# The shift layer of a four-layer network on one core: four positions per tile, its group norm computed once, its statistics taken inside the layer before

## The chip, the core and the metric

The kernel runs on one core of a Trainium2 chip (trn2). A core has a matrix engine (TensorE, PE in the profile; its weight loads are listed apart as PEld), a vector engine (VectorE, DVE), a scalar engine (ScalarE, ACT), a general engine (GpSimd, POOL) and a queue engine (SyncE, SP). SBUF is the on-chip memory of 128 partitions; PSUM is the memory that TensorE writes and that POOL does not read here. DMA transfers are issued by SP or ACT and run on 16 DMA engines that all queues share. The metric is the device time of one execution in microseconds; lower is better. All data is 32-bit floating point.

## What is computed

Eight images of 384 channels and 32 x 32 pixels pass through four residual layers. Layers 0 and 2 are selective state-space layers (layer 2 ends in an MLP), layer 1 is a deformable convolution. The change concerns layer 3, the shift layer, and the end of layer 2.

```python
def _gn(v, G=32, eps=1e-5):
    B_, C_, H_, W_ = v.shape
    g = v.reshape(B_, G, C_ // G, H_, W_)
    m = jnp.mean(g, axis=(2, 3, 4), keepdims=True)
    s = jnp.var(g, axis=(2, 3, 4), keepdims=True)
    return ((g - m) / jnp.sqrt(s + eps)).reshape(v.shape)

def _L3_conv_ref(x, offset):
    B, C, h, w = x.shape
    P = offset.shape[0]                      # 48 positions
    cpp = C // P                             # 8 channels each
    off_round = jnp.round(offset)
    off_int = off_round.astype(jnp.int32)
    disp = _displace(x.reshape(B, P, cpp, h, w), off_int).reshape(B, C, h, w)
    sub = offset - lax.stop_gradient(off_round)
    c = K // 2                               # K = 5, SIGMA = 0.5
    jj, ii = jnp.meshgrid(jnp.arange(K, dtype=jnp.float32) - c, jnp.arange(K, dtype=jnp.float32) - c, indexing='xy')
    field = jnp.stack([jj, ii], axis=-1)
    d = field[None] + sub[:, None, None, :]
    kernel = jnp.exp(-jnp.sum(d * d, axis=-1) / (2.0 * SIGMA ** 2))
    kernel = kernel / jnp.sum(kernel, axis=(1, 2), keepdims=True)
    kw = jnp.repeat(kernel, cpp, axis=0)[:, None]
    return lax.conv_general_dilated(disp, kw, (1, 1), [(c, c), (c, c)],
        feature_group_count=C, dimension_numbers=('NCHW', 'OIHW', 'NCHW'))

x = x + _L0_conv_ref(_gn(x), ...)
x = x + _L1_conv_ref(_gn(x), ...)
x = x + _L2_conv_ref(_gn(x), ...)
x = x + _L3_conv_ref(_gn(x), L3_conv_offset)
```

Each position has an offset (dx, dy) that its eight channels share. The channels are moved by the rounded offset, with zeros from outside, and then blurred with a 5 x 5 Gaussian centred on the fractional rest. Shift and blur along one axis are one 32 x 32 matrix, so a position needs two small matrices: one over y, one over x.

## The kernel before, in words

**Layer 2.** `ssm_layer` works through 16 steps, a half image each (`b`, `h`; 384 channels as three groups of 128 partitions, 512 pixels). A step is 48 units (six channel groups of the inner state by eight pairs of states). The order of ACT, PE, DVE and POOL is written out by hand: `plan` puts each operation into one of four queues at a unit number, and `run` issues them between the scans. SP is not in that list, so its transfers are ordered by the scheduler. The B and C rows of the next step come from DRAM in eight transfers of 1 MB (`load_bc`, L367) into eight buffers called `bc`, put at units 41 to 48. The MLP of a step runs among the units of the next one, except for the last step: there `out_proj`, `mlp_up`, `gelu` and `mlp_down` stand alone at the end of `ssm_layer`. `down_take` (L545, L547) adds the result to the residual `x` on DVE, and `store` (L504) writes the half image to DRAM after the third group. The weights of these products stream through three buffers `wm` (L246).

**Layer 3.** `shift_layer` opens new buffers and starts when layer 2 is done.
1. From the offsets it makes the rounded part, the fraction and the normaliser (L1402 to L1424).
2. For each of the eight images it loads `x` (L1432, two buffers), takes bn_stats of six 128 x 512 pieces (L111), aggregates (L125), and runs `gn_finish`: a product with `gmat` that averages the 12 channels of a norm group (L133), the deviations and their squares, a second product (L143), and Ln and Exp for the reciprocal root (L174, L175). The result is a scale and a shift per image and channel, `rn`.
3. Six products (L1444) spread scale and shift into `tab`, one value for each partition, image and channel slot.
4. In the loop over the 48 positions a tile `xr` holds one position: partition = (channel within a group of four, y), columns = (8 images, 2 channel groups, 32 x). It comes in two loads on SP of 128 KB (L1475) into three buffers. DVE scales and shifts it (L1481, two operations), TensorE multiplies four 128-column blocks of the data, as the stationary operand, with the block-diagonal matrix over y (L1490), which also turns the block; ACT copies the result out of PSUM (L1492); four more products do the x axis and turn it back (L1495); DVE adds it to `xr` (L1497); ACT issues two stores of 128 KB (L1500). The matrices of four positions at a time are built in the same loop on DVE and ACT (L1459 to L1468).

In DRAM the images lie as [image, channel, pixel], so loads and stores of a position move runs of 32 pixels, 128 bytes.

Of the kernel before, what the change touches and what calls it, by code (L numbers as in the profile page):

```python
# [8 lines left out]
F32 = mybir.dt.float32  # L9
# [75 lines left out]
class Net:  # L85
# [107 lines left out]
    def ssm_layer(self, li, src, dst):  # L193
# [3 lines left out]
        with ExitStack() as ctx:  # L197
# [292 lines left out]
            def residual(s):  # L490
                s["x"] = x = p2.tile([P, G, TS], F32, name="x", tag="x")
                nc.sync.dma_start(out=x, in_=src(s["b"])[:, :, s["sl"]])
# [9 lines left out]
            def store(s, o):  # L502
                if o == G - 1:
                    nc.sync.dma_start(out=dst(s["b"])[:, :, s["sl"]], in_=s["x"])  # L504
# [135 lines left out]
            with tc.manual_schedule(engines=ENGINES):  # L640
# [75 lines left out]
                residual(s)  # L716
                for o in range(G):
                    out_proj(s, o, 0, ND)
                    out_take(s, o)
                if mlp:  # L720
                    for q in range(NF // 4):
                        for f in range(4):
                            mlp_up(s, q, f)
                            up_take(s, q, f)
                        gelu(s)
                        for o in range(G):
                            mlp_down(s, q, o)
                            down_take(s, q, o)

# [653 lines left out]
    def shift_layer(self, src_of, src, dst):  # L1383
        tc, nc, ins = self.tc, self.nc, self.ins
        nb = self.nb
        NJ = CPP // IG
        NC4 = C // IG
        with ExitStack() as ctx:
            wp = ctx.enter_context(tc.tile_pool(name="w3", bufs=1))
            p2 = ctx.enter_context(tc.tile_pool(name="p2_3", bufs=2))  # L1390
            self.mm = ctx.enter_context(tc.tile_pool(name="mm3", bufs=3, space=PSUM))
            self.acc = ctx.enter_context(tc.tile_pool(name="acc3", bufs=3, space=PSUM))
            cst = wp.tile([P, T_D0 + W], F32, name="cst")
            nc.sync.dma_start(out=cst, in_=ins["c_l3"])
            off = wp.tile([P, NP, 2], F32, name="off")
            nc.sync.dma_start(
                out=off.rearrange("p n t -> p (n t)"),
                in_=ins["offset"].rearrange("n t -> (n t)").partition_broadcast(P),
            )

            offf = off.rearrange("p n t -> p (n t)")
            nc.vector.tensor_scalar(offf, offf, 4096.0, -4096.0, ALU.min, ALU.max)  # L1402
            rnd = wp.tile([P, NP, 2], F32, name="rnd")
            rndf = rnd.rearrange("p n t -> p (n t)")
            nc.vector.tensor_scalar(rndf, offf, ROUND, None, ALU.add)
            nc.vector.tensor_scalar(rndf, rndf, ROUND, None, ALU.subtract)
            sub = wp.tile([P, NP, 2], F32, name="sub")
            nc.vector.tensor_tensor(sub, off, rnd, ALU.subtract)
            norm = wp.tile([P, 2 * NP], F32, name="norm")
            tap = wp.tile([P, 2 * NP], F32, name="tap")  # L1410
            subf = sub.rearrange("p n t -> p (n t)")
            for t in range(-2, 3):
                nc.vector.tensor_scalar(tap, subf, float(t), None, ALU.add)
                nc.vector.tensor_tensor(tap, tap, tap, ALU.mult)
                dest = norm if t == -2 else tap
                nc.scalar.activation(dest, tap, AF.Exp, scale=-2.0)
                if t > -2:
                    nc.vector.tensor_tensor(norm, norm, tap, ALU.add)
            nc.vector.reciprocal(norm, norm)

            pos = wp.tile([P, 2 * NP], F32, name="pos")
            nc.vector.tensor_scalar(pos, rndf, self.col(Q_SRC + NT), None, ALU.add)
            nc.vector.scalar_tensor_tensor(norm, pos, 0.0, norm, ALU.is_ge, ALU.mult)
            nc.vector.scalar_tensor_tensor(norm, pos, float(W - 1), norm, ALU.is_le, ALU.mult)  # L1424
            grp = cst[:, T_GRP : T_GRP + IG]
            d0 = cst[:, T_D0 : T_D0 + W]


            rn = wp.tile([P, 2, nb, G], F32, name="rn")
            for b in range(nb):  # L1430
                x = p2.tile([P, G, L], F32, name="x", tag="x")
                nc.sync.dma_start(out=x, in_=src_of(b))  # L1432
                self.gn_stats(x, rn[:, 0, b, :], rn[:, 1, b, :])
            nq = P // IG
            hi = cst[:, T_HI : T_HI + nq].unsqueeze(1).to_broadcast([P, nb, nq])
            tab = wp.tile([P, 2, G, nb, nq], F32, name="tab")
            for t in range(2):
                for g in range(G):
                    sel = p2.tile([P, nb, nq], F32, name="sel", tag="sel")
                    nc.vector.tensor_tensor(  # L1440
                        sel, hi, rn[:, t, :, g].unsqueeze(2).to_broadcast([P, nb, nq]), ALU.mult
                    )
                    ps = self.psum("ps_tab", n=nb * nq)
                    nc.tensor.matmul(  # L1444
                        ps, cst[:, T_LO : T_LO + P], sel.rearrange("p b q -> p (b q)"), start=True, stop=True
                    )
                    nc.scalar.copy(tab[:, t, g].rearrange("p b q -> p (b q)"), ps)

            PC = 4
            for p0 in range(0, NP, PC):  # L1450
                M2 = 2 * PC
                e = p2.tile([P, M2, W], F32, name="e", tag="e")
                kr = p2.tile([P, M2, W], F32, name="kr", tag="kr")
                ef, krf = e.rearrange("p m w -> p (m w)"), kr.rearrange("p m w -> p (m w)")

                def rows(t):
                    return t[:, 2 * p0 : 2 * p0 + M2].unsqueeze(2).to_broadcast([P, M2, W])

                nc.vector.tensor_tensor(e, d0.unsqueeze(1).to_broadcast([P, M2, W]), rows(rndf), ALU.add)  # L1459
                nc.vector.tensor_tensor(kr, e, rows(subf), ALU.add)  # L1460
                nc.vector.tensor_tensor(krf, krf, krf, ALU.mult)
                nc.scalar.activation(krf, krf, AF.Exp, scale=-2.0)
                nc.scalar.activation(ef, ef, AF.Abs)
                nc.vector.scalar_tensor_tensor(krf, ef, 2.0, krf, ALU.is_le, ALU.mult)
                nc.vector.tensor_tensor(kr, kr, rows(norm), ALU.mult)
                bd = p2.tile([P, M2, IG, W], F32, name="bd", tag="bd")
                for i in range(IG):
                    nc.scalar.activation(bd[:, :, i, :], kr, AF.Copy, scale=grp[:, i : i + 1])  # L1468
                for n in range(PC):
                    p = p0 + n  # L1470
                    g, q = divmod(p * NJ, nq)
                    xr = p2.tile([P, nb, NJ, W], F32, name="xr", tag="xr", bufs=3)
                    for j in range(NJ):
                        c = p * CPP + j * IG
                        nc.sync.dma_start(  # L1475
                            out=xr[:, :, j, :],
                            in_=src[:, c : c + IG, :].rearrange("b i (y x) -> (i y) b x", x=W),
                        )
                    xa = p2.tile([P, nb, NJ, W], F32, name="xa", tag="xa")
                    for op, t in ((ALU.mult, 0), (ALU.add, 1)):  # L1480
                        nc.vector.tensor_tensor(  # L1481
                            xa, xr if t == 0 else xa,
                            tab[:, t, g, :, q : q + NJ].unsqueeze(3).to_broadcast([P, nb, NJ, W]), op,
                        )
                    xaf = xa.rearrange("p b j x -> p (b j x)")
                    my = bd[:, 2 * n + 1].rearrange("p i w -> p (i w)")
                    mx = bd[:, 2 * n].rearrange("p i w -> p (i w)")
                    ps = self.acc.tile([P, HL], F32, name="ps_y", tag="acc")
                    for k in range(0, HL, P):
                        nc.tensor.matmul(ps[:, k : k + P], xaf[:, k : k + P], my, start=True, stop=True)  # L1490
                    yt = p2.tile([P, HL], F32, name="yt", tag="yt")
                    nc.scalar.copy(yt, ps)  # L1492
                    ps2 = self.acc.tile([P, HL], F32, name="ps_yx", tag="acc")
                    for k in range(0, HL, P):
                        nc.tensor.matmul(ps2[:, k : k + P], yt[:, k : k + P], mx, start=True, stop=True)  # L1495
                    xrf = xr.rearrange("p b j x -> p (b j x)")
                    nc.vector.tensor_tensor(xrf, xrf, ps2, ALU.add)  # L1497
                    for j in range(NJ):
# [98 lines left out]
```

## Time and profile before

| | us |
|---|---|
| median of 3 runs | 9791.53 (9788.88 to 9793.73) |
| the profiled execution | 9790.55 |
| its span, first to last instruction | 9788.6 |
| last take of the last MLP ends | 9418.7 |
| last issue of a store ends | 9785.2 |

| engine | busy us | share of the span |
|---|---|---|
| PE | 8670.8 | 89% |
| DVE | 8165.1 | 83% |
| ACT | 6591.8 | 67% |
| POOL | 5655.4 | 58% |

Most of the span is layers 0 to 2, where several engines are nearly full at once. The rows used below come from views with these columns. In a windows view each row is a stretch of the span: its length, then the busy time of each engine with the number of instructions, the granted TensorE clock (1 is full speed), the mean busy share of the 16 DMA engines, and GB/s. In the chain of waits each row is a start time, a length and what the program's end was waiting for then. In a table of groups each row is a line, engine, operation, output<-input, shape and count, then total busy time, mean nanoseconds of one, and the idle time ahead of it with what ended it.

### The profile page before, as it was taken

The page shows a single profiled execution, that of the slowest core. Times are in us where ns is not written, and L with a number is a line of the kernel's source. Part 1 is how long each engine was busy: PE and PEld are TensorE (multiplying, and loading weights), DVE is VectorE, ACT ScalarE, POOL GpSimd, SP SyncE. Part 2 cuts the span into 40 slices and gives each one's busy share as a digit, 9 for nine tenths or more (in the row PEclk, how much of TensorE's full clock was granted, in tenths as well). Part 3 has the DMA queues.
Part 4 walks back from the last instruction along what each step waited for, and adds up shares of the span by engine and source line. Part 5 has one row for each costly group of instructions (what it writes and reads, how often), then busy time and mean ns, then how long its engine had stood idle before and what let it go on. Part 6 is the DMA issues. An engine that isn't in the chain of part 4 may idle for free. (4 is left out here: it accounts for less than half of the span.)

```text
span 9788.6 us, 89617 instructions
## 1 busy us (share of the span) xinstructions
PE 8670.8 (89%) x28965; PEld 4696.1 (48%) x28990; DVE 8165.1 (83%) x8959; ACT 6591.8 (67%) x10417; POOL 5655.4 (58%) x3740
## 2 busy tenths in 40 slices
PE   7888898888886999999999996899999999999876
PEld 2333333333333777767767774333344343443345
DVE  6999999999995778777877875999999999999834
ACT  5666666666663778777777775777767777677632
POOL 6888888888883000000000001999999999999900
PEclk8999999999998999999999997899999999999976
DMA  2211211211212333333333333222332223322226
GB/s 75 77 57 45 82 58 45 82 57 45 82 48 54 78 85 73 91 87 74 90 89 77 85 84 96 72 86 87 112 104 91 86 88 115 101 91 85 74 85 100
DMA packets 540008, 781.12 MB, mean 80 GB/s; under 512 B 231858, under 2 KB 372562, under 8 KB 515848
## 3 DMA queue, kind: packets, MB, share of 16 engines
q1 hardware_dynamic: 439688, 762.71, 26.4%
q10 hardware_dynamic: 99840, 12.59, 0.8%
q8 instruction: 231, 3.78, 0.2%
q14 instruction: 249, 2.04, 0.1%
HBM read 717.32 MB, written 57.87 MB: 79 GB/s over the span
## 5 line engine op out<-in xcount | busy, mean ns | idle before, releaser
L426 POOL TENSOR_TENSOR db<-du,bc 128x1024 f32<-128x1024 f32 x1536 | 3608.1, 2354 | 420.2 <-DVE hs L436 227.4
L436 DVE TENSOR_TENSOR_SCAN da<-da,db 128x1024 f32<-128x1024 f32 x1272 | 2912.3, 2290 | 200.1 <-ACT da L421 151.3
L467 PE MATMUL y<-hs,ident 128*128 128x512 f32 x5184 | 2611.1, 639 | 389.6 <-DVE hs L450 246.5
L421 ACT ACTIVATE da<-dt,na 128x512 f32<-128x512 f32 x3072 | 2120.2, 691 | 911.9 <-DVE hs L450 685.4
L394 POOL TENSOR_TENSOR dt<-dt,sp_e 128x512 f32<-128x512 f32 x192 | 243.8, 1270 | 3089.5 <-DVE sp_e L386 3089.5
L467 PEld LDWEIGHTS y<-hs,ident 128*128 128x128 f32 x5184 | 1018.6, 203 | 1877.6 <-issue 1138.4
L1370 PE MATMUL wacc<-fsm,fxk 128*128 128x221 f32 (+34 forms) x10624 | 1637.2, 312 | 73.4 <-DVE fsm L1340 71.6
L450 DVE TENSOR_TENSOR hs<-da,bc 128x1024 f32<-128x1024 f32 x1272 | 1558.0, 1225 | 117.7 <-PE y L467 14.1
L1370 PEld LDWEIGHTS wacc<-fsm,fxk 128*128 128x128 f32 x10624 | 1550.2, 193 | 210.2 <-DVE fsm L1340 132.6
L1340 DVE TENSOR_TENSOR fsm<-fhy,fhx 128x170 f32<-128x170 f32 (+42 forms) x3216 | 1174.2, 431 | 429.6 <-PE wacc L1370 414.1
L1300 ACT ACTIVATE fhy<-fpyx,cell 128x416 f32<-128x416 f32 (+9 forms) x1280 | 645.6, 576 | 397.9 <-DVE fsm L1340 397.9
L1058 PE MATMUL ps_off<-fxn,fow 128*32 128x248 f32 (+18 forms) x2944 | 832.7, 523 | 3.8 <-issue 2.0
L1323 DVE TENSOR_TENSOR fxk<-fxt,fwk 128x1024 f32<-128x1024 f32 (+1 forms) x688 | 787.5, 1182 | 6.3 <-ACT fxt L1116 6.3
L436 DVE TENSOR_TENSOR_SCAN hs<-da,db 128x1024 f32<-128x1024 f32 x264 | 602.4, 2282 | 67.7 <-POOL db L414 27.8
L447 POOL TENSOR_TENSOR hs<-hs,bc 128x1024 f32<-128x1024 f32 x264 | 621.7, 2355 | 38.0 <-ACT st L442 37.5
L454 POOL TENSOR_TENSOR hs<-hs 128x512 f32<-128x512 f32 x480 | 608.6, 1268 | 3.6 <-DVE hs L450 3.6
L538 PE MATMUL ps_m<-hid,wm 128*128 128x512 f32 x1152 | 540.4, 614 | 38.8 <-ACT hid L531 33.9
L521 PE MATMUL ps_h<-t,wm 128*128 128x512 f32 x1152 | 539.0, 606 | 15.0 <-DVE x L545 15.0
L1305 ACT ACTIVATE fhy<-fhy,cols 128x1344 f32<-128x1344 f32 (+10 forms) x368 | 530.7, 1442 | 12.0
L1058 PEld LDWEIGHTS ps_off<-fxn,fow 128*98 128x98 f32 (+2 forms) x2944 | 352.7, 147 | 382.2 <-issue 359.4
L442 ACT COPY st<-da 128x2 f32<-128x2 f32 x624 | 97.8, 157 | 504.4 <-DVE hs L450 503.0
L538 PEld LDWEIGHTS ps_m<-hid,wm 128*128 128x128 f32 x1152 | 222.2, 196 | 342.7 <-issue 263.6
(182 smaller groups left out, 9871.1 us busy)
## 6 DMA issues: line engine op xcount, KB each, us to landing
bc<-bcd SPq DMA_DIRECT2D x256, 1024.0 KB
fpyx<-fposd SPq DMA_DIRECT2D x640, 256.0 KB
wm<-in_w SPq DMA_DIRECT2D x96, 768.0 KB
x<-x SPq DMA_DIRECT2D x72, 768.0 KB
winr<-in_win SPq DMA_DIRECT2D x192, 192.0 KB
x<-in_x SPq DMA_DIRECT2D x40, 768.0 KB
fpyx<-fposd SPq DMA_DIRECT2D x24, 1024.0 KB
wm<-in_wout SPq DMA_DIRECT2D x48, 384.0 KB
```

What stands on the lines that cost most here:

```text
L421: nc.scalar.activation(da[:, i, :], s["dt", j], AF.Exp, scale=na[:, j, n : n + 1])
L426: nc.gpsimd.tensor_tensor(db, du, s["bc"][m][:, 0], ALU.mult)
L436: nc.vector.tensor_tensor_scan(h1, da1, db1, 0.0, ALU.mult, ALU.add)
L447: nc.gpsimd.tensor_tensor(s["hs", m], s["hs", m], c, ALU.mult)
L450: nc.vector.tensor_tensor(hs, s["da", m], c, ALU.mult)
L467: nc.tensor.matmul(s["y"], self.ident, s["hs", m][:, i, :], start=first and i == 0, stop=k == NU - 1 and i == n - 1,)
L538: nc.tensor.matmul(ps, s["w2"][:, f, o * P : (o + 1) * P], s["hid"][:, f, :], start=(f == 0), stop=(f == 3))
L1058: nc.tensor.matmul(o[:, ya - r0 : yb - r0, xa:xb], ow[:, (dy + pad) * K + dx + pad, :], x3[:, ya + dy : yb + dy, xa + dx : xb + dx], start ...
L1300: nc.scalar.activation(hy[:, at : at + (yb - ya) * W], pyx[:, 0, ya * W : yb * W], AF.Abs, bias=bias)
L1323: nc.vector.tensor_tensor(t[:, :n], x, wk[:, j : j + 1, :].to_broadcast([P, n, P]), ALU.mult)
L1340: nc.vector.tensor_tensor(self.sub(sm, at, [(r * w, n), (w, r), (1, w)]), self.sub(hy, hy_at[by] + xa, [(r * W, n), (W, r), (1, w)]), self ...
L1370: nc.tensor.matmul(a[:, ya - 4 * o : yb - 4 * o, xa:xb], k, self.sub(sm, sm_at[by], [(w, yb - ya), (1, w)]), start=False, stop=False,)
```

## The change

The shift layer is no longer a layer with its own buffers: `shift_parts` returns pieces that `ssm_layer` issues within its last MLP and after it, in the buffers of layer 2 (`bc`, `hs`, `db`, `u`, `xn`).

- `store` of layer 2 writes every third of a half image also to a new DRAM tensor `x3s` laid out [channel, y, image, x], in one transfer of 128 x 16 runs of 128 bytes; the old copy is written too, except in the last step.
- Ahead of the last `out_proj` six half images are loaded for the statistics; `kernels_a`, `kernels_b` and the bn_stats of 15 half images (five after each `gelu`) stand among the MLP's operations, and those of the last half image after each of its takes, from SBUF.
- `norms` does the two averaging products once, with the eight images side by side as columns, and builds `tab` with three products.
- A tile is now four positions: partition = (position, y), columns = (8 channels, 8 images, 32 x), 1 MB, loaded from `x3s` in four transfers of 1 KB runs. A chunk is half a tile, 128 x 1024. POOL multiplies by the scale; TensorE multiplies with the block-diagonal y matrix as the stationary operand and adds the shift as a second product of the same matrix with a broadcast row of the table; DVE transposes 32 x 32 blocks out of PSUM; TensorE does x; DVE transposes back; POOL adds. 32 stores of 32 KB a tile, half on SP, half on ACT.

The core of the diff, with the parts the text speaks of:

```diff
             def store(s, o):
-                if o == G - 1:
+                if mlp:
+                    y = s["h"] * H // 2
+                    nc.sync.dma_start(
+                        out=shift[0][o * P : (o + 1) * P, y : y + H // 2, s["b"] * W : (s["b"] + 1) * W],
+                        in_=s["x"][:, o, :].rearrange("p (y x) -> p y x", x=W),
+                    )
+                if o == G - 1 and (not mlp or s is not steps[-1]):
                     nc.sync.dma_start(out=dst(s["b"])[:, :, s["sl"]], in_=s["x"])
...
                 residual(s)
+                if mlp:
+                    load_consts()
+                    last = len(steps) - 1
+                    for i in range(6):
+                        stat_load(i)
+                    stats = list(range(last))
                 for o in range(G):
                     out_proj(s, o, 0, ND)
                     out_take(s, o)
                 if mlp:
+                    kernels_a()
...
                         gelu(s)
+                        if q == NF // 4 - 1:
+                            exp_ln()
+                        some(5)
+                        if q == 0:
+                            kernels_b()
                         for o in range(G):
                             mlp_down(s, q, o)
                             down_take(s, q, o)
+                            if q == NF // 4 - 1:
+                                stat(last, s["x"], o)
+                    for m in range(3):
+                        load(m)
+                    norms()
+                    main()
...
+        def bc(name, *shape):
+            t = ring("bc", [P, 2, 2, TS], name, NS // 2).rearrange("p a b l -> p (a b l)")
...
+        def load(m):
+            xr = d["xr", m] = bc("sxr", NI, W).rearrange("p (i w) -> p i w", w=W)
+            for n in range(IG):
+                c = (m * IG + n) * CPP
+                nc.sync.dma_start(
+                    out=xr[n * H : (n + 1) * H].rearrange("p (k b) w -> p k (b w)", k=CPP),
+                    in_=srcs[c : c + CPP].rearrange("k y b -> y k b"),
+                )
...
+        def scale(c):
+            m = c // 2
+            if c % 2 == 0:
+                d["xa", m] = bc("sxa", NI, W).rearrange("p (i w) -> p i w", w=W)
+            x, xa = (piece(d[k, m], c).rearrange("p (i w) -> p i w", w=W) for k in ("xr", "xa"))
+            nc.gpsimd.tensor_tensor(xa, x, table(c, 0).unsqueeze(2).to_broadcast([P, NI // 2, W]), ALU.mult)
+        def over_y(c):
+            ps = d["psy", c] = dap.tile([P, 2, TS], F32, name="ps_y", tag="da")...[:, :CH]
+            xa = piece(d["xa", c // 2], c)
+            for i in range(0, CH, HL):
+                o = ps[:, i : i + HL]
+                nc.tensor.matmul(o, mat(c, 1), xa[:, i : i + HL], start=True, stop=False)
+                t = table(c, 1)[:, i // W : i // W + HL // W].unsqueeze(2).to_broadcast([P, HL // W, W])
+                nc.tensor.matmul(o.rearrange("p (i w) -> p i w", w=W), mat(c, 1), t, start=False, stop=True)
+        def turn(c):
+            yt = d["yt", c] = ring("hs", [P, 2, TS], "syt", 4).rearrange("p a b -> p (a b)")
+            nc.vector.transpose(yt, d["psy", c])
+        def over_x(c):
+            d["psx", c] = []
+            for i in range(0, CH, HL):
+                ps = self.psum("ps_yx")
+                nc.tensor.matmul(ps, mat(c, 0), d["yt", c][:, i : i + HL], start=True, stop=True)
+                d["psx", c].append(ps)
+        def turn_back(c):
+            zt = d["zt", c] = ring("db", [P, 2, TS], "szt", 3).rearrange("p a b -> p (a b)")
+            for i, ps in enumerate(d["psx", c]):
+                nc.vector.transpose(zt[:, i * HL : (i + 1) * HL], ps)
+        def add(c):
+            m = c // 2
+            x = piece(d["xr", m], c)
+            nc.gpsimd.tensor_tensor(x, x, d["zt", c], ALU.add)
+            if c % 2:
+                for k in range(CPP):
+                    for n in range(IG):
+                        (nc.sync if n % 2 else nc.scalar).dma_start(
+                            out=dst[:, (m * IG + n) * CPP + k, :].rearrange("b (y x) -> y b x", x=W),
+                            in_=d["xr", m][n * H : (n + 1) * H, k * nb : (k + 1) * nb, :],
+                        )
+        def main():
+            nch = 2 * NM
+            for i in range(-3, nch):
+                for k, fn in ((3, scale), (2, over_y), (1, over_x), (2, turn), (1, turn_back), (0, add)):
+                    if 0 <= i + k < nch:
+                        fn(i + k)
+                m = i // 2 + 3
+                if i % 2 and 3 <= m < NM:
+                    load(m)
```

## Prediction

> **What bounds the kernel now.** I read the windows view by stage first, then the chain of waits from 9300 us to the end, then the timeline of each engine and the DMA view of the last stage. The four stretches below are the last MLP, the statistics of the shift layer, its tables, and its 48 positions.
>
> ```profile
> core 0: us, PE busy (x) PEld busy (x) DVE busy (x) ACT busy (x) POOL busy (x), PEclk, DMA share, GB/s
> 9327.00:9419.00 92.00, 81.50 (x181) 34.94 (x179) 7.82 (x11) 17.01 (x19) 0.00 (x0) 0.96 0.17 53
> 9419.00:9530.00 111.00, 63.18 (x286) 62.10 (x287) 46.25 (x139) 37.51 (x80) 0.00 (x0) 0.52 0.39 129
> 9530.00:9543.00 13.00, 9.19 (x39) 6.80 (x39) 7.15 (x14) 5.27 (x13) 0.00 (x0) 0.67 0.00 0
> 9543.00:9789.00 246.00, 160.61 (x744) 141.90 (x744) 105.75 (x175) 49.97 (x103) 0.00 (x0) 0.64 0.65 100
> ```
>
> The MLP is bound by TensorE (81.5 of 92 us) and leaves DVE, ACT and DMA nearly empty. The next 370 us have no busy engine: POOL does nothing, the granted clock is 0.52 and 0.64. Nothing before 9327 us is touched but the stores of layer 2. The chain says what the 370 us wait for:
>
> ```profile
> 9464.33 4.02 PE gn_ps L143 x18
> 9468.53 2.97 DVE gn_st L111 x5
> 9471.77 3.98 PE gn_ps L133 x18
> 9476.73 4.01 PE gn_ps L143 x18
> ...
> 9606.26 2.73 DMA out<-xr
> 9609.52 2.49 DMA xr<-x
> 9612.21 0.59 ACT yt L1492
> 9612.84 2.09 PE ps_yx L1495 x8
> 9614.96 0.70 DVE xr L1497
> 9616.15 3.89 DMA out<-xr
> 9620.57 3.60 DMA xr<-x
> ```
>
> In the statistics each of eight samples pays two rounds of 18 passes of tiny matmuls, 4 us each, and its own DVE work, one after another. In the positions the chain goes store, load, multiply, store: three xr buffers make a load wait for an earlier store. 246 us for 48 positions is 5.1 us each.
>
> **The statistics go into the last MLP.** The change loads 15 half samples of 768 KB early, and puts their 45 bn_stats (0.68 us by L111, 30.6 us) and the aggregates (24 of 0.17, 4 us) between the MLP's takes, along with the kernel matrices: some 13 DVE operations of 0.2 to 0.75 us and four of 768 elements at about 0.95 (between 0.69 at 512 and 1.23 at 1024), 8 us; on ACT some 3.4 and 3.7 us. The timeline of DVE shows idle stretches of 33.7, 16.0 and 17.5 us before the three groups of takes; the loads are 11.8 MB in some 120 us at a DMA share of 0.17. So I cost it at nothing; uncovered it would be 31 + 4 + 8 + 7 = 50 us. The risk is SP's queue: loads 6 to 14 wait for DVE and could stand ahead of the MLP's weights (L246). I allow 0 to 5 us, take 1. What stays behind the last take (ends 9418.7) is one bn_stats and an aggregate, 0.85.
>
> **One group norm for all.** 18 passes of matmul (3.98), four small DVE operations (1.1), 18 passes (4.0), Ln and Exp and the bias (0.8), six `sel` of 0.42 (2.5), then the table product and its copies, of which the first multiply needs about the first (1.7 + 0.6). With the allowance the first multiply starts at 9435.2; POOL's 2.35 later, at 9437.6, TensorE starts. Gone with it are the other seven rounds and 15 table loads of 1.28 (L174, L175).
>
> **The positions.** They become 24 chunks of 128x1024, two to a tile of four positions. The prices are:
>
> ```profile
> L426 POOL TENSOR_TENSOR db<-du,bc 128x1024 f32<-128x1024 f32 x1536 | 3608.1, 2354 | 420.2 <-DVE hs L436 227.4
> L436 DVE TENSOR_TENSOR_SCAN da<-da,db 128x1024 f32<-128x1024 f32 x1272 | 2912.3, 2290 | 200.1 <-ACT da L421 151.3
> L450 DVE TENSOR_TENSOR hs<-da,bc 128x1024 f32<-128x1024 f32 x1272 | 1558.0, 1225 | 117.7 <-PE y L467 14.1
> ...
> q10 hardware_dynamic: 99840, 12.59, 33.8%
> q1 hardware_dynamic: 93600, 11.80, 30.7%
> ```
>
> (The last two rows are the DMA queues over 9543:9789: packets, MB, share of 16 engines.) For a tile, two chunks:
> - TensorE: six products of 512 columns a chunk. In the MLP 24 passes (12 products) take 10.3 us, so a pass is 0.43 and a product two: 12 x 0.43 x 2 = 10.3 us at full clock.
> - POOL: multiply and add, 2 x 2 x 2.354 = 9.4 us.
> - DVE: the block transposes have no row. At one element a cycle like L450 (1.23 for 1024, 0.68 for each of two 512) it is 5.2 us, at the scan's two cycles 9.4. I take 5.2, since a transpose has one operand and no recurrence; either is below TensorE.
> - DMA: the store stays at 128-byte packets: 0.338 x 16 x 246 / 99840 = 13.3 ns each, 8192 of them 6.8 us on 16 engines. The load has 1 KB packets, no row: between 2.4 us (441 GB/s, the fastest slice of the old statistics loads) and 6.6 us (8192 packets at 12.9 ns, the present load's). I take 2.9, near the large loads, since its packets are eight times those of now: together 9.7, at the worst 13.4.
> - Issue: 16 stores on ACT at 0.44 are 7.1 us; 16 stores and 4 loads on SP at 0.36 to 0.48 are 7.2 to 9.6. ACT has nothing else to do.
>
> Five resources lie between 7 and 10.3, so none will run quite full: I take 11.0 a tile, 10.3 as the floor, 13.4 as the bound if DMA decides. From 9437.6, chunk 1 is added after 5.1 (a first product group half cold) + 3.4 + 1.7 + 3.4 + 1.7 + 0.7 + 2.4 = 18.4 us, at 9456.0. Eleven tiles more end at 9577.0. The last tile's stores need 16 issues (7.1) and the 3.4 us between the last issue now (9785.2) and the span's end: **9587.5**. The profiled execution took 1.95 us more than its span, and the median is 1 us above it, so the forecast is **9590**, 2.1% less.
>
> **The stores of layer 2.** Each of 16 steps adds three stores of 2048 packets of 128 B, 1.7 us of DMA each, issued by SP and waiting for the takes at L545 and L547. Behind them in SP's queue are the B and C loads (L367) and weights. Those loads are put four units ahead of use, and a unit is 4.1 us in DVE's timeline; the waits view of 6200 to 9300 lists no compute engine waiting for a DMA among its 37 longest. So nothing; uncovered 16 x 3 x 1.7 = 82 us.
>
> **The Trainium skill against it.** The trace says first: two stores of 128 KB leave ACT's queue in 1.01 us, without waiting for each other. "DMA: Bandwidth & Descriptors", section Bandwidth, says that "Transfers under 64 KB are descriptor-dominated", and gives 0.68 us for 4 KB and 0.95 for 64 KB; the change cuts 96 stores of 128 KB into 384 of 32 KB. By an estimate from that page, at 0.8 us for one and none overlapping, a tile would need 25.6 us instead of 11 and the kernel would take about 9760. On the clock, the trace has 0.64 with gaps of 1 to 3 us between groups of 8 passes, and 0.96 in the MLP with gaps up to 4. "TensorE: Matmul & The Clock Gate", section Part 1, lets the clock fall after an idle window of about 3.4 us; by it the dense pipeline here stays at full clock, and if starved, passes would be 0.86.
>
> **Rivals.**
> 1. The loads stand behind the stores. `load(m + 3)` comes after the stores of m and is needed two chunks later. If SP keeps that order, a tile takes 16 x 0.46 + 4 x 0.48 of issue, some 5 until the load lands, and 4.7 for multiply and add: 19 us. 9456.0 + 11 x 19 + 10.5 + 3 = **9678**; with the clock half down (20.6 us of passes) 9696. For it: the program's order, and 1 MB landings. Against: eight buffers with five or six in use, and SP's queue now shows loads moved ahead of other work (xr loads at 9424.7 among the statistics loads).
> 2. The cover in the MLP is thin: statistics or weights late. The bn_stats alone exposed: 9590 + 31 = **9621**.
> 3. Slower: each 32 KB store holds its queue until it lands. At the 2.7 us of the short store pieces in the chain, 16 per queue are 43 us a tile: 9456.0 + 12 x 43 + 3 = **9975**. It decides from (9788.6 - 10.5 - 9456.0) / 11 = 29 us a tile, or 1.8 us a store. For it: stores and loads are 46% of that stage's chain. Against: two issues in 1.01 us, and 33.8% of all DMA engines on one queue.
> 4. It doesn't do what it says: the positions keep waiting for their stores, now two tiles' worth; that is between 1 and 3.
>
> **How the numbers follow.** Forecast (10.3 to 12.5 us a tile, 9580 to 9607): 0.57. Rival 1 and its half measures (12.5 to 20.6, 9607 to 9696): 0.25. Rival 2 (9607 to 9640): 0.09. Rival 3: 0.05. Below 9580: 0.02; about as before: 0.02. The range 9572 to 9680 leaves out rival 3, no change and the far end of rival 1, about 0.12. A run tells a difference of 0.2% (20 us) from none. Faster by more: 0.57 + 0.25 + 0.09 + 0.02 = 0.93; within: 0.02; slower: 0.05.
>
> **What would show it.** A last MLP of 92 us still; first `ps_y` product near 9438; a granted clock above 0.9 and TensorE over 85% busy in the last stage; POOL the next; transposes of 128x1024 near 1.2 us. Rival 1 shows as POOL's multiply waiting for xr, and rival 3 as issue times on ACT and SP far above 0.5 us. The prediction is wrong if a tile takes over 13.4 us or layer 2 gets longer.

## The result, and the profile after

The changed kernel takes **9634.76 us** (median of 4 runs, 9633.36 to 9640.38) against 9791.35 us of the kernel before beside it: ratio 0.9841, 95% interval 0.9824 to 0.9858. So it is faster by 1.6% where 2.05% was forecast: 9590 lies 45 us below. The profiled execution took 9640.38 us, with a span of 9638.6.

First the windows view of the changed kernel. The MLP with the statistics in it is the first row shown, the first three tiles the second, tiles 3 to 11 the third.

```profile
core 0: us, PE busy (x) PEld busy (x) DVE busy (x) ACT busy (x) POOL busy (x), PEclk, DMA share, GB/s
9327.00:9419.00 92.00, 82.56 (x182) 35.67 (x182) 45.63 (x101) 24.30 (x29) 0.00 (x0) 0.95 0.45 145
...
9435.00:9464.00 29.00, 29.00 (x69) 12.58 (x67) 12.51 (x15) 0.59 (x1) 15.78 (x8) 1.00 0.57 101
9464.00:9609.00 145.00, 100.12 (x193) 41.68 (x192) 40.07 (x50) 0.00 (x0) 67.05 (x32) 0.86 0.63 117
```

VectorE's work in the MLP rose from 7.8 to 45.6 us, and TensorE's 82.6 us in the same 92 shows that nothing was slowed by it. For 29 us the new last stage runs as designed: TensorE never idle, clock 1.00. Then TensorE falls to 69% busy, and no engine is full: POOL has 67 of 145 us, the DMA engines 0.63. The statistics' 111 us and the tables' 13 have become 16 us, as TensorE's timeline shows (start, length, idle before):

```profile
9421.62 1.74 PE L1523 MATMUL gn_ps<-smv,gmat 128*128 128x16 f32 x14 [1.40 <-DVE smv L1514]
9424.31 3.91 PE L1539 MATMUL gn_ps<-sdm,gmat 128*128 128x8 f32 x18 [0.95 <-DVE sdm L1535]
9429.73 5.28 PE L1562 MATMUL ps_tab<-ssel,cst 128*128 128x512 f32 x6 [1.51 <-DVE ssel L1553]
9434.85 1.02 PE L1602 MATMUL ps_y<-sxa,sbd 128*128 128x512 f32 x2
```

What TensorE waits for is POOL's multiply (L1592), the first of a tile, and what that waits for is in POOL's timeline:

```profile
9452.03 1.91 POOL L1592 TENSOR_TENSOR sxa<-sxr,stab 128x1024 f32<-128x1024 f32 x1
...
9464.52 1.91 POOL L1592 TENSOR_TENSOR sxa<-sxr,stab 128x1024 f32<-128x1024 f32 x1 [7.37 <-DMA out<-sxr]
...
9482.10 1.91 POOL L1592 TENSOR_TENSOR sxa<-sxr,stab 128x1024 f32<-128x1024 f32 x1 [9.20 <-DMA out<-sxr]
...
9500.43 1.91 POOL L1592 TENSOR_TENSOR sxa<-sxr,stab 128x1024 f32<-128x1024 f32 x1 [9.95 <-DMA out<-sxr]
...
9518.64 1.91 POOL L1592 TENSOR_TENSOR sxa<-sxr,stab 128x1024 f32<-128x1024 f32 x1 [9.83 <-DMA out<-sxr]
```

From the fourth tile on the multiplies of two tiles stand 18.1 us apart (9464.52 to 9609.03 for eight tiles). The view puts most of these waits down to a store, one of them (9554.56) to the load `sxr<-x3s`. The multiply waits for the four loads of its tile: at 9482 the semaphores that POOL waits for are the four that these loads had taken. (A semaphore is a counter that a transfer raises when it has landed.) Their place shows in SP's queue (x is the number of transfers):

```profile
9460.72 11.87 SPq L1629 DMA_DIRECT2D out<-sxr  x16
9472.68 4.82 SPq L1573 DMA_DIRECT2D sxr<-x3s  x4
9477.60 12.90 SPq L1629 DMA_DIRECT2D out<-sxr  x16
9490.77 5.05 SPq L1573 DMA_DIRECT2D sxr<-x3s  x4
```

This is a closed loop, and its parts add up to a tile. The multiply of tile 3 starts at 9464.52; the addition of tile 1's second chunk comes behind it on POOL and ends at 9468.7 (4.2 us); the last eight of tile 1's stores on SP are issued by 9472.6 (3.9); the four loads of tile 4 behind them by 9477.5 (4.9); they land at 9482.0 (4.5), and the multiply of tile 4 starts. 17.5 us the first time, 18.3 the next.

A row of the queue holds both the issuing and the waiting between two issues. The first two lines are the issues alone (least, median and longest ns of one). The next three are what SP's queue waited for in the eight tiles from 9464 to 9609 (us in total, times, longest):

```profile
L1629 SPq DMA_DIRECT2D out<-sxr x167: 315/450/812, 9460.7 to 9630.0; - x167
L1573 SPq DMA_DIRECT2D sxr<-x3s x34: 303/403/465, 9459.8 to 9603.8; - x34
```

```profile
SPq L1573 <- DMA out<-sxr: 27.6, 11, 4.1
SPq L1629 <- DMA out<-sxr: 21.2, 23, 1.5
SPq L1629 <- POOL sxr L1625: 19.6, 8, 3.2
```

The issues of a tile take 16 x 0.45 + 4 x 0.40 = 8.8 us. Waiting for earlier stores to land takes (27.6 + 21.2) / 8 = 6.1, waiting for the addition 2.5. So of the 17.4 us that SP needs for a tile, about half is issuing.

By stages, against the prediction: the first multiply came at 9432.5 instead of 9435.2 (-2.7), chunk 1 was added at 9452.1 instead of 9456.0 (-1.2 more), the other eleven tiles took 177.3 us instead of 121 (+56.3), and the tail 9.2 instead of 10.5 (-1.3): 51.1 us in all, the difference of the spans (9638.6 and 9587.5).

### The profile page after: what moved, and what is told of

It reads as the page before. It is cut to its first block, busy times and chain, and to the rows that moved or that the text cites. A ratio compares the mean times of both kernels' runs of the same rounds, so it can differ in the third digit from the quotient of the medians.

```text
span 9638.6 us, 87976 instructions
## 1 busy us (share of the span) xinstructions
PE 8594.0 (89%) x28252; PEld 4554.4 (47%) x28252; DVE 8105.5 (84%) x8807; ACT 6508.4 (68%) x10236; POOL 5755.9 (60%) x3788
```

## Experiments

The 9400 us ahead of the first multiply vary by up to 13 us between executions of versions that are the same there (it came between 9419.3 and 9432.5). So the last stage is compared by itself: from the first multiply to the end of the span.

| version | time us | ratio (interval) | first multiply | last stage us | a tile us |
|---|---|---|---|---|---|
| the prediction | 9590 | | 9435.2 | 152.3 | 11.0 |
| the change | 9634.76 | 0.9841 (0.9824 to 0.9858) | 9432.50 | 206.1 | 18.1 |
| loads early | 9616.67 | 0.9821 (0.9804 to 0.9837) | 9427.73 | 187.1 | 15.8 |
| all stores on ACT | 9655.97 | one run | 9429.43 | 224.6 | 10.3, then stores |
| no shift product | 9633.81 | one run | 9430.53 | 201.5 | 18.1 |
| half the stores | 9603.53 | one run | 9427.82 | 173.9 | 15.4 |
| loads early, 10 of 32 stores on SP | 9592.69 | 0.9801 (0.9785 to 0.9817) | 9419.25 | 164.6 | 13.0 |
| 10 of 32 stores on SP, loads late | 9623.24 | 0.9836 (0.9820 to 0.9852) | 9424.96 | 195.9 | 16.3 |
| 8 stores a tile, loads early | 9574.64 | 0.9779 (0.9763 to 0.9796) | 9434.20 | 141.9 | 10.85 |
| 8 stores a tile, loads late | 9572.17 | 0.9782 (0.9765 to 0.9798) | 9434.48 | 141.8 | 10.85 |
| loads on POOL's queue | 9589.63 | 0.9793 (0.9777 to 0.9809) | 9428.24 | 156.0 | 12.2 |
| statistics behind the MLP | 9678.63 | one run | 9467.89 | 208.9 | 18.3 |

### The loads earlier

```diff
             for i in range(-3, nch):
+                m = i // 2 + 3
+                if i % 2 == 0 and 3 <= m < NM:
+                    load(m)
                 for k, fn in (...):
...
-                m = i // 2 + 3
-                if i % 2 and 3 <= m < NM:
-                    load(m)
```

In SP's queue the loads of tile m + 3 now stand ahead of the stores of tile m instead of behind them.

> The load of tile m + 3 is put one chunk earlier, ahead of the addition of tile m's first half, so that SP issues it before that tile's stores. Theory A (the loads stand behind the stores in SP's order, and a tile of 18.1 us is multiply and add 4.2, the second half's stores 4.4, the issue of the loads 5, their landing 4.6): a tile falls to 11 to 13 us, the kernel to 9585 to 9600. Theory B (the number of transfers bounds: 36 a tile, eight in flight, some 4 us each): a tile stays near 18, the kernel within 10 us of 9635. Theory C (TensorE bounds): no change.

Measured: 9616.67, 15.8 us a tile; between the two theories. The last stage is 19 us shorter, so the loads' place was part of it, but the multiply still waits 7 to 8 us. SP's queue of this version shows why:

```profile
9480.86 9.69 SPq L1629 DMA_DIRECT2D out<-sxr  x16
9490.88 4.07 SPq L1573 DMA_DIRECT2D sxr<-x3s  x4
9495.97 10.50 SPq L1629 DMA_DIRECT2D out<-sxr  x16
9506.51 4.29 SPq L1573 DMA_DIRECT2D sxr<-x3s  x4
```

10 us for the stores and 4 to 5 for the loads, with 0 to 1 us between the rows: SP issues or waits nearly all the time, for 15.8 us a tile. The prediction had 7.2 to 9.6 for the issues, and the issues alone are again about 9 (medians of 0.45 us each). Of the 90 us from 9470 to 9560, 35 are waits of this queue for an earlier transfer to land, 6.2 us a tile.

### All stores on ACT's queue

```diff
-                        (nc.sync if n % 2 else nc.scalar).dma_start(
+                        nc.scalar.dma_start(
```

> All 32 stores of a tile are issued by ACT, SP has only the loads. A: the loads no longer stand behind stores, but ACT needs 32 x 0.46 = 15 us a tile and twice as long at the end; about 15.5 a tile, the kernel near 9620. B: unchanged at 18 a tile or a little worse, 9635 to 9645. C: no change.

Measured: 9655.97, slower than the change, and none of the three expected times. POOL's timeline has no wait for a load up to 9500, and ACT's queue is the last to end:

```profile
9484.94 1.91 POOL L1592 TENSOR_TENSOR sxa<-sxr,stab 128x1024 f32<-128x1024 f32 x1
9490.03 1.91 POOL L1592 TENSOR_TENSOR sxa<-sxr,stab 128x1024 f32<-128x1024 f32 x1
9495.24 1.91 POOL L1592 TENSOR_TENSOR sxa<-sxr,stab 128x1024 f32<-128x1024 f32 x1
9500.33 1.91 POOL L1592 TENSOR_TENSOR sxa<-sxr,stab 128x1024 f32<-128x1024 f32 x1
```

```profile
9503.17 136.89 ACTq L1629 DMA_DIRECT2D out<-sxr  x264
```

With the loads alone on SP the arithmetic runs at 5.15 us a chunk, 10.3 a tile, the predicted floor, until all buffers wait for stores. The stores leave one queue at 136.89 / 264 = 0.52 us each; 384 of them need about 200 us, and they end the kernel. Theory A had 0.46 us each and 9620.

### Without the shift's product

```diff
-                nc.tensor.matmul(o, mat(c, 1), xa[...], start=True, stop=False)
-                t = table(c, 1)[...]
-                nc.tensor.matmul(o..., mat(c, 1), t, start=False, stop=True)
+                nc.tensor.matmul(o, mat(c, 1), xa[...], start=True, stop=True)
```

The norm's shift is left out: a third of TensorE's passes in this stage.

> The second product of each 512 columns over y, which adds the group norm's shift, is left out: 4 of 12 passes fewer a chunk, 3.4 us of TensorE a tile. A and B: TensorE waits anyway in the steady part; only the fill of the pipeline and the last chunk gain some 3 to 5 us, the kernel near 9631. C: 3.4 us for each of 12 tiles, 9594.

Measured: 9633.81, 18.1 us a tile. TensorE isn't what sets the tile.

### Half of the stores

```diff
-                for k in range(CPP):
+                for k in range(0, CPP, 2):
```

Every second channel isn't stored; the loads and the arithmetic are complete.

> Every second channel of a tile is not stored, 16 stores of 32 KB a tile instead of 32. A: the second half's stores ahead of the loads take 2.2 instead of 4.4 and the loads' issue 4 instead of 5; about 15 a tile, the kernel near 9605. B: half the transfers, about 10.5 a tile where TensorE takes over, 9570 to 9580. C: no change but the last stores, 9631.

Measured: 9603.53, 15.4 us a tile, near theory A's 15 and far from theory B's 10.5. Half of the stores, with their bytes and packets, away takes 2.7 us off a tile; the rest of the loop stays. Where bytes had decided, a tile would have come near TensorE's 10.3.

### The stores split 10 to 22, with the loads early

```diff
-                        (nc.sync if n % 2 else nc.scalar).dma_start(
+                        (nc.sync if n == 1 or (n == 3 and k % 4 == 0) else nc.scalar).dma_start(
```

> Early loads as in the run with the loads one chunk earlier (tile 15.8 us, 9616.7), and the 32 stores of a tile split 10 on SP's queue and 22 on ACT's, in place of 16 and 16, so that SP, which also issues the 4 loads, is relieved. Theory D (the issue on the queue decides: 0.54 us a store on a queue, from 384 stores in about 204 us on one queue): ACT 22 x 0.54 = 11.9 us a tile, SP 10 x 0.54 plus 4 loads at 0.5 to 1.1 = 7.4 to 9.8; the tile falls to 12 to 12.5 us, the kernel to 9580 to 9595. Theory E (what decides is that the two queues together have only eight transfers under way: 36 transfers in 15.8 us are 0.44 us each, whichever queue issues them): the tile stays at 15 to 16, the kernel at 9610 to 9622. Theory A alone (loads late, nothing else): no change against the run with early loads either, but with the multiply still waiting for its loads.

Measured: 9592.69, 13.0 us a tile (9483.93 to 9548.78 for the last five). Theory D's 9580 to 9595 holds; the tile is 0.5 above its 12 to 12.5, and theory E's 15 to 16, a fixed 0.44 us for each transfer, falls. The same 36 transfers of the same bytes on the same two queues, six of them moved, take 22.5 us off the last stage. The queues, ACT's first:

```profile
9479.79 50.22 ACTq L1629 DMA_DIRECT2D out<-sxr  x88
```

```profile
9495.74 6.01 SPq L1629 DMA_DIRECT2D out<-sxr  x10
9501.79 5.35 SPq L1573 DMA_DIRECT2D sxr<-x3s  x4
```

Now both issue or wait nearly all the time: ACT 50.22 / 88 = 0.57 us a store, 22 of them 12.6 us; SP 6.0 + 5.3 = 11.3, of which its 14 issues are under 6 (medians 0.45 and 0.31 us). That ACT's 12.6 sets the tile is read from these rows; no run shows it by itself.

### The same split with the loads behind the stores

The split of the last diff alone, on the change.

> The change with only the stores' split undone from 16 and 16 to 10 on SP and 22 on ACT; the loads stay behind the stores. Loads' place and queue's issue add up (theory A with D): in the change a tile's 18.1 us are multiply and addition 4.2, the stores behind the second addition 4.4, issue of the loads 5, landing 4.6; with 5 stores instead of 8 behind the second addition 2.7 to 3 for 4.4, tile 16 to 17, kernel 9610 to 9625. Were SP's load alone the cause (D without A), tile 12 to 13.5 and 9585 to 9597 as with early loads. If the loads' place alone counted (A without D), no change: 9630 to 9640.

Measured: 9623.24, 16.3 us a tile, in the bounds of "loads' place and queue's issue add up". Its last stage of 195.9 us is 10 shorter than the change's; its ratio alone can't be told from the change's. Together with the two runs before: the loads' place is worth 19 us with the stores 16 to 16 and 31 with them 10 to 22; the split 10 us with late loads and 22.5 with early ones. Both act on SP's queue.

### The loads on POOL's queue

```diff
         def load(m):
...
-                nc.sync.dma_start(
+                nc.gpsimd.dma_start(
```

> The change with its four loads a tile issued by POOL's queue instead of SP's; place in the program, stores (16 on SP, 16 on ACT) and all else as in the change. On POOL the loads stand behind the second addition and ahead of the multiply after it, with no store before them. Queue theory (A with D: the tile is long since SP issues 20 of 36 transfers and the loads stand behind SP's stores): the stores need 16 x 0.52 to 0.57 = 8.3 to 9.1 us a queue, so TensorE sets the tile, 10.3 to 11.5 us, the last stage (first multiply to the end of the span) 145 to 165 us, the kernel 9575 to 9595, plus what the issue costs POOL: POOL has 8.5 of 10.3 us busy, so more than 0.45 us for each load would show, and at 1 us each the tile is 12.5 and the kernel about 9605. Theory G (the transfers of all queues hold each other up, whichever queue issues them): the loads' landing and the stores stay as slow as with loads early on SP, the tile 14 to 18, the last stage 180 to 206 us.

Measured: 9589.63, 12.2 us a tile, last stage 156.0 us: one word takes 50 of the 206 us away, to within 4 us of the predicted 152.3. Theory G falls. The word changes more than the issuing queue: in the DMA view the loads now move in packets of 3.3 KB (2,880 for 9.44 MB) instead of 1 KB. But they land no sooner for it, 5.1 us after their issue (median) against some 4.5 above. SP's queue, now with stores alone, still waits 40.8 of the 98 us from 9455 to 9553 for transfers to land; no load stands behind these waits any more. POOL's timeline shows what the tile is now made of (the additions stand between the lines):

```profile
9504.09 1.91 POOL L1592 TENSOR_TENSOR sxa<-sxr,stab 128x1024 f32<-128x1024 f32 x1 [1.62 <-PE ps_y L1604]
...
9508.25 2.34 POOL L1573 DMA_DIRECT2D sxr<-x3s  x4
9510.59 1.92 POOL L1592 TENSOR_TENSOR sxa<-sxr,stab 128x1024 f32<-128x1024 f32 x1
...
9516.51 1.91 POOL L1592 TENSOR_TENSOR sxa<-sxr,stab 128x1024 f32<-128x1024 f32 x1 [1.69 <-DMA sxr<-x3s]
```

Issuing four loads keeps POOL for 2.34 us, 0.59 each; with 8.5 us of multiplies and additions it is at 10.9, and a wait of 1 to 2 us for the landing is left.

### Eight stores a tile instead of 32

```diff
-                out=xr[n * H : (n + 1) * H].rearrange("p (k b) w -> p k (b w)", k=CPP),
-                in_=srcs[c : c + CPP].rearrange("k y b -> y k b"),
+                out=xr[:, n * 2 * nb : (n + 1) * 2 * nb].rearrange("p (j b) w -> p j (b w)", j=2),
+                in_=srcs[c : c + CPP].rearrange("(j i) y b -> (i y) j b", i=IG),
...
-            if c % 2:
-                for k in range(CPP):
-                    for n in range(IG):
-                        (nc.sync if n % 2 else nc.scalar).dma_start(
-                            out=dst[:, (m * IG + n) * CPP + k, :].rearrange("b (y x) -> y b x", x=W),
-                            in_=d["xr", m][n * H : (n + 1) * H, k * nb : (k + 1) * nb, :],
+            for n in (0, 1):
+                for j in (0, 1):
+                    ch = (m * IG + c % 2 * 2 + n) * CPP + j * IG
+                    k = (c % 2 * 2 + n) * 2 + j
+                    (nc.sync if j else nc.scalar).dma_start(
+                        out=dst[:, ch : ch + IG, :].rearrange("b i (y x) -> (i y) b x", x=W),
+                        in_=d["xr", m][:, k * nb : (k + 1) * nb, :],
```

The four blocks of 32 partitions hold four channels of one position, as in the kernel before, and the positions lie beside each other; the stationary matrix then belongs to 512 columns instead of to the tile, and each tile's matrices are made two chunks ahead. Loads early.

> The same work with four channels of one position in a partition block, as in the kernel before, instead of four positions: a store is 128 KB of 128 partitions and a tile has 8 of them instead of 32 (and 4 loads of 256 KB as now), with the same bytes in runs of 128; the matrices are stationary for 512 columns as now, and those of a tile are made two chunks ahead instead of all at once. Loads early. Theories D and E (the number of transfers decides): 12 transfers a tile instead of 36, so TensorE sets the tile, 10.3 to 11 us; the kernel at 9570 to 9590. Theory F (the packets and bytes decide, not the number of transfers): the tile stays at 14 to 16 us, the kernel at 9605 to 9625. Where the matrices made on the fly get in the way of VectorE, 1 to 2 us a tile more than by D.

Measured: 9574.64, 10.85 us a tile, by theories D and E; F falls. Its windows view, and three multiplies in a row from its POOL timeline, without a wait:

```profile
9464.00:9570.00 106.00, 99.26 (x227) 41.97 (x225) 92.36 (x92) 24.46 (x60) 82.93 (x38) 1.00 0.79 161
```

```profile
9464.79 2.09 POOL L1604 TENSOR_TENSOR sxa<-sxr,stab 128x1024 f32<-128x1024 f32 x1
...
9469.95 2.09 POOL L1604 TENSOR_TENSOR sxa<-sxr,stab 128x1024 f32<-128x1024 f32 x1
...
9475.64 2.10 POOL L1604 TENSOR_TENSOR sxa<-sxr,stab 128x1024 f32<-128x1024 f32 x1
```

TensorE is 94% busy at clock 1.00. Chunks take 5.15 and 5.7 us in turn; the 0.55 over TensorE's 5.15 is there in every second chunk, and by the timeline VectorE, which has 92 of 106 us, is then late with a transpose. SP's queue waits for no transfer to land (9460 to 9560), only for the additions and, 3.9 us in all, for TensorE. What the DMA engines moved was hardly different. The two queues of the change from 9435 to 9639, and then of this version from 9435 to 9577 (packets, MB, share of 16 engines; q1 is SP's, q10 ACT's):

```profile
q1 hardware_dynamic: 62511, 16.22, 40.3%
q10 hardware_dynamic: 52224, 6.30, 21.3%
```

```profile
q1 hardware_dynamic: 58689, 14.74, 45.2%
q10 hardware_dynamic: 49920, 6.29, 28.4%
```

108,609 packets instead of 114,735, in 142 us instead of 204. The packets of the stores stayed at 128 bytes; the number of transfers that carry them fell, from 36 to 12 a tile. With it a store came to leave 128 partitions instead of 32, which no run takes apart from their number.

### The same with the loads behind the stores

The diff of the loads, undone on this version.

> The version with four channels of a position in a block (8 stores of 128 KB a tile, 9574.6 us) with its loads put back where the change has them: behind the stores of the odd chunk. If the loads' place is a cause by itself, whatever the number of stores, the multiply waits again: the loads are issued when the addition of the odd chunk is over, and the multiply that needs them follows two POOL chunks (about 8 to 10 us) later, so with 2 stores (1.0 us) and 4 loads (1.8) to issue and 4.6 us to land there are 0 to 2 us of wait a tile: 9575 to 9595. If the loads' place costs what it cost with 32 stores (2.3 us a tile between the change and its early version): about 9595. If the number of stores ahead of the loads is the whole of it: within 5 us of 9574.6.

Measured: 9572.17, and a last stage of 141.8 us against 141.9. With two stores ahead of them (1.0 us in SP's queue) it doesn't matter where the loads stand. The last of the three conditions holds.

### The statistics behind the MLP

```diff
-                        some(5)
...
-                            if q == NF // 4 - 1:
-                                stat(last, s["x"], o)
+                    some(last)
+                    for o in range(G):
+                        stat(last, s["x"], o)
```

> The change with one part undone: all of layer 2's statistics are taken after the last MLP instead of within it; stores, loads and tiles are those of the change. The prediction's step (the statistics cost nothing within the MLP, about 1 us): the 48 takes come back as time of their own, 31 us of bn_stats at least and about 50 with their waits, so the kernel at 9666 to 9690. Rival (the cover was thin: they slowed the MLP by much of what they saved): the MLP gets shorter than 92 us by the same, and the kernel comes to 9640 to 9655.

Measured: 9678.63. The windows of this version:

```profile
9327.00:9419.00 92.00, 82.51 (x180) 35.81 (x181) 14.05 (x32) 24.31 (x29) 0.00 (x0) 0.95 0.29 85
9419.00:9480.00 61.00, 25.49 (x71) 15.14 (x70) 40.00 (x88) 2.26 (x5) 7.52 (x4) 0.64 0.62 155
```

In the MLP VectorE has 14 us instead of 45.6, and TensorE has the same 82.5 in the same 92: the statistics cost the MLP nothing. From the last take to the first multiply it is 46.6 us (9421.25 to 9467.89) instead of 12.6 (9419.91 to 9432.50), so the cover is worth 34.0. The prediction had 31 + 4 = 35 us for these two kinds of instruction (the 8 and 7 us for the matrices stay in the MLP here).

## Why the prediction fell 45 us short

- **Statistics within the MLP cost nothing**: right. Both windows of 92 us have TensorE at 82.5, and uncovered they cost 34.0.
- **One group norm, first multiply at 9435.2**: right to 2.7 us. The first 14 of 18 tiny matmuls took 1.74 us, not 3.98; the second round 3.91, as costed.
- **TensorE 10.3 us a tile, transposes at one element a cycle**: right. The transposes of 128x1024 took 1.25 us and those of 512 0.675, and the undisturbed tiles run at 10.3.
- **POOL 9.4 us**: 8.5. The multiply by a broadcast table took 1.91 us instead of 2.354, the addition 2.34.
- **Stores of layer 2 cost nothing**: right. From the first to the last of layer 2's 96 matmuls of the mean it is 2943.4 us, before 2943.7.
- **DMA 9.7 us a tile, at the worst 13.4**: not the bound. The version with 8 stores moves the same bytes in 10.85 us a tile at a share of 0.79.
- **Issue, "16 stores and 4 loads on SP at 0.36 to 0.48 are 7.2 to 9.6"**: right for the issues themselves, 8.8 us a tile. The step that failed is the one from this term to 11.0 us a tile: the prediction counted SP as one of "Five resources" that "lie between 7 and 10.3", with no waits between its issues and no loop through its queue. SP also waited 6.1 us a tile for earlier stores to land and 2.5 for the addition, 17.4 in all, and the loads stood at the end of it. On ACT a store took 0.52 to 0.57 us in a steady row instead of 0.44.
- **Rival 1, the loads behind the stores**: its mechanism happened, at 18.1 us a tile instead of 19, and its mark, POOL's multiply waiting for xr, is the chief wait of the profile. The kernel came to 9635 instead of its 9678 since the first three tiles, loaded ahead, run at 10.3. Of the evidence weighed against it, "SP's queue now shows loads moved ahead of other work" was no evidence for this loop: in the changed kernel the loads stand behind the 16 stores, where the program puts them.
- **Rivals 2 and 3**: both fall. No store holds its queue until it lands; at 0.57 a store stays far below the 1.8 us from which that rival decides.
- **Rival 4, the positions still waiting for their stores**: in part. The loads do wait for stores to land, 27.6 us in eight tiles, but the result lies on the fast side of rival 1, not between rivals 1 and 3.
- **TensorE over 85% busy, clock above 0.9**: seen for the first three tiles (100%, 1.00), not after (69%, 0.86). That lower clock isn't on the path: with a third of the passes left out the tile stays at 18.1.

So the missing time is nearly all one loop: the four loads of a tile are issued by a queue that already has 16 stores to issue, behind those stores, with waits for earlier transfers between the issues, and the loop closes once a tile. Of the 53.8 us by which the last stage is longer than predicted, 50.1 go when the loads are issued on POOL's queue instead of SP's. 19.0 go with their place in it alone, and 41.5 with their place and six stores fewer on it. How the rest divides between SP's issues and its waits for landings, no run shows.

"DMA: Bandwidth & Descriptors", in its section "Issuing engines are not separate DMA queues", says that spreading transfers over issuing engines saves only the sequencer's time to start them, "which is usually small relative to the DMA itself". Here the choice of the engine wasn't small: six stores moved from SP to ACT were worth 22.5 us, waits in the queue included. The estimate from its section Bandwidth, 25.6 us of stores for a tile and 9760 for the kernel, was too dear: the two queues sent 32 small stores in the 13.0 us of a tile. That small transfers are worth avoiding is what the 8-store version shows, though not by the size of the packets, which stayed the same.

## What to carry to other kernels

Count the transfers of a steady stage on each issuing queue and price them by a steady row of such transfers, with the waits between them, not by a pair that stands alone: here a queue of 20 small transfers set the pace while every engine and the DMA engines had time to spare. Where a load stands behind a store that waits for arithmetic, and that arithmetic stands in an engine's program behind one that waits for an earlier load, add up the loop; its length is the stage's pace. Fewer and larger transfers of the same packets removed both questions here: the four-channel layout with 8 stores takes 9574.6 us, 60 us less than the change.

## What the runs showed that was not expected

- A steady row of stores of 32 KB leaves one queue at 0.52 us each (264 in 136.9 on ACT) or 0.57 (88 in 50.2 with SP at work beside it), though the change's chain of waits has single issues of 0.46.
- In the change, loads wait for stores of other tiles, even for stores on the other queue. The buffer that a load fills was emptied by stores a whole tile earlier. But in the trace the transfers of SP and ACT share eight semaphores, and 335 of the 337 issues from 9446 to 9609 wait for the one that they take themselves, so for an earlier transfer to land. The second load of tile 4, for one, is issued at 9476.18, 3.1 us after the first has been: its semaphore had been taken by a store of ACT at 9473.79. By this at most eight transfers of the two queues are under way at a time; no run changes that number.
- POOL's multiply by a broadcast table takes 1.91 us where the addition of two full operands of the same 128x1024 takes 2.34.
- The block transposes of VectorE (PSUM to SBUF, four bytes) run at the pace of a copy: 1.25 us for 1024 columns, 0.675 for 512.
- In the version with 8 stores two operations of 128x256 on VectorE (L1498 and L1507, which make the matrices) take 2.45 us each beside a POOL that is 78% busy, 42 of VectorE's 92 us. In the same kernel's MLP, with POOL idle, they take 0.42. POOL's multiply takes 2.09 there instead of 1.91. No run takes the two engines apart.
